# Two attention layers on one core: position products and q's transposes moved to the middle of score blocks, v's bias and two sums rearranged

## The chip, the cores and the metric

The kernel runs on one core of one Trainium2 chip. The metric is device time in microseconds, the median of several executions; lower is better. One execution was also profiled, and every duration below comes from that profile. The engines are named as the profile names them: PE is TensorE (PEld its weight loads), DVE is VectorE, ACT is ScalarE, POOL is GpSimd, SP issues most of the DMAs.

## The reference

Four images of 32x32 positions and 768 channels pass through two attention layers, each with 12 heads of 64 channels. Cut to what matters:

```python
def layer0(x):                       # x: (4, 1024, 768), after a group norm without weights
    q, k, v = heads(x@Wq + bq), heads(x@Wk + bk), heads(x@Wv + bv)
    attn = q @ k.T / 8 + rel_h(q)[..., None] + rel_w(q)[..., None, :]
    return softmax(attn) @ v  @ Wp + bp
def layer1(x):
    q, k, v = (layer_norm(dwconv3x3(s)) for s in split(x @ w_qkv.T + b_qkv))   # per head
    attn = q @ k.T / 8 + rel_h(q) + rel_w(q)
    return (softmax(attn) @ v + q) @ w_proj.T + b_proj
x = x + layer0(group_norm(x));  x = x + layer1(group_norm(x))
```

`rel_h` and `rel_w` are products of each query with a table of relative positions, 32 rows and 32 columns per query, added to every score.

## The kernel before, in words

**Stages and pairs.** The work is cut into eight stages (image, layer), in the order (0,0), (1,0), (0,1), (1,1), (2,0), (3,0), (2,1), (3,1), and each stage into six pairs of heads [...]. That makes 48 pairs, numbered 0 to 47: pairs 0 to 11 and 24 to 35 are of layer 0, the others of layer 1. All arithmetic is fp32.

**The run of a pair.** `attend` computes one pair's softmax attention for 1024 queries. It goes through four blocks: two halves of 512 queries (chunk c), and in each half two groups of four key tiles (g = 0 and 4). A block is: four score tiles (each four `s<-q,k` and two `s<-bias,ones` matmul records, the latter adding the relative positions), each followed by an `e` exponential on ACT over 128x1024 values; sums of the four exponentials into `acc` on DVE; then sixteen `av` matmul records that apply the exponentials to `vt`. Score tiles have two PSUM buffers, so the third tile of a block needs the first exponential done.

**A half's tail.** When a half's second block is over, ACT copies `av` to `weighed`, and the parts `sums` (a `z` matmul pair on PE, then `t`, Ln and Exp on ACT) and `result` (DVE: two Newton operations, then the product with `weighed`, put in place of q) are queued in `rest`. `more()` takes the next part of `rest`, once after the scores of each block and once after its `av`.

**Making the next pair meanwhile.** `attend` is a generator with four yields in a block, two after the scores and two after `av`; each yield is one step, so a run has 16. While pair i-1 runs, the pieces of pair i are emitted at the steps that `Pair.plan` gives, steps 4k and 4k+1 after the scores of block k, 4k+2 and 4k+3 after its `av`. All of PE, DVE, ACT and POOL work in exactly the order in which the program emits (a manual schedule). So the plan is the only scheduler: an instruction that waits holds up all behind it on its engine.

- Layer 0 (from pair 2 on): `sevens(Q)` makes the q and k products of a pair by a seven-product scheme from sums of quarters of the tokens (`mix_tokens`, DVE, in `quarters` and in place in `xn`), `sevens(V)` those of v for two pairs.
- Layer 1: `padded` (product of 24 matmul records `qkv`, then ACT writes a padded image), `taps` (nine DVE operations of 1.3 us), `centre` (32 `ln_c` records; ACT squares and copies), `squares` (a DVE reduction), `norm` (Ln and Exp on ACT, then DVE), `back` (four transposes `ln_t`, then ACT writes q and the reordered copy `q_t`, or k). The padded q of pair i+1 begins in the second half of run i-1, at its steps 8 and 10.
- Both: `positions(0)` and `positions(1)` (128 short `rel` records each, then two ACT copies into `whole`), and `split` (ACT casts `whole` to `high`, DVE subtracts, POOL issues 16 DMAs that spread both into the `bias` tiles).

**PSUM.** Two score tiles take four banks, `av` one, and the other three are one ring: every `bank(...)` call takes the next of the three, whatever it is for (`z`, `qkv`, `ln_c`, `ln_t`, `rel`, `proj` ...), and its first matmul waits until the tile three calls earlier has been read.

**Projection.** `project` handles a finished stage during the first run of the next: six output tiles, each with two halves of 24 `proj` records; DVE adds bias and residual. For image 0 each output tile first computes `pbias`, the projection of v's bias plus the projection's bias (12 records of one column), in both layers.

Of the kernel before, what the change touches and what calls it, by code (L numbers as in the profile page):

```python
# [45 lines left out]
def two_layers(ctx: ExitStack, tc: tile.TileContext, keep, x_in, wqkv, wproj, rels, windows, vrow, small, const, onehot, picks, out):  # L46
# [231 lines left out]
    sk = fixed.tile([P, NSMALL], F32, tag="sk", name="sk")  # L278
    nc.vector.tensor_scalar(sk, sm, SCALE, None, ALU.mult)

    pbias = fixed.tile([P, 2, NC], F32, tag="pbias", name="pbias")

    ones = fixed.tile([P, T], F32R, tag="ones", name="ones")
    plain = one.tile([P, T], F32, tag="whole", name="plain")
# [8 lines left out]
    class Pair:  # L293
# [253 lines left out]
        def plan(self):  # L547

            Q, K, V = 0, 1, 2
            if not self.layer and not in_sevens(self.i):  # L550
                return [
                    (0, lambda: self.plain(Q, 0)),
                    (2, lambda: self.plain(Q, 1)),
                    (4, lambda: self.plain(K, 0)),
                    (5, lambda: self.positions(0)),
                    (6, lambda: self.plain(K, 1)),
                    (7, lambda: self.positions(1)),
                    (8, lambda: self.plain_v(0)),
                    (10, lambda: self.split()),
                    (10, lambda: self.plain_v(1)),  # L560
                ]
            if not self.layer:
                pieces = [
                    (0, lambda: self.sevens(Q, False)),
                    (2, lambda: self.sevens(Q, True)),
                    (6, lambda: self.positions(0)),
                    (8, lambda: self.positions(1)),
                    (10, lambda: self.split()),
                ]
                if self.hp % 2 == 0:  # L570
                    pieces += [(8, lambda: self.sevens(V, False)), (10, lambda: self.sevens(V, True))]
                return [(r + shift(self.i), piece) for r, piece in pieces]

            pieces = [
                (-8, lambda: self.padded(Q, 0)),
                (-6, lambda: self.padded(Q, 1)),
                (-4, lambda: self.padded(K, 0)),
                (-2, lambda: self.padded(K, 1)),
                (2, lambda: self.padded(V, 0)),
                (4, lambda: self.padded(V, 1)),  # L580
                (3, lambda: self.centre(Q)),
                (5, lambda: self.squares(Q)),
                (7, lambda: self.norm(Q)),
                (8, lambda: self.centre(K)),
                (9, lambda: self.back(Q, 0)),
                (9, lambda: self.back(Q, 1)),
                (10, lambda: self.squares(K)),
                (10, lambda: self.positions(0)),
                (11, lambda: self.positions(1)),
                (12, lambda: self.norm(K)),  # L590
                (12, lambda: self.split()),
                (13, lambda: self.centre(V)),
                (14, lambda: self.back(K, 0)),
                (14, lambda: self.back(K, 1)),
                (14, lambda: self.squares(V)),
                (15, lambda: self.norm(V)),
            ]

            taps = (
                (Q, -4, (2, 2, 2, 2, 1)),  # L600
                (K, 2, (2, 2, 2, 2, 1)),
                (V, 8, (2, 2, 3, 2)),
            )
            for s, r, counts in taps:
                lo = 0
                for n in counts:
                    pieces.append((r, lambda s=s, lo=lo, n=n: self.taps(s, lo, lo + n)))
                    r, lo = r + 1, lo + n
            return pieces


# [2 lines left out]
    def attend(pair, os):  # L614
# [12 lines left out]
        for c in range(T // QC):  # L627
# [24 lines left out]
            def result(weighed, t, inv, cols=cols):  # L652

                nc.vector.scalar_tensor_tensor(t, t, -1.0, inv, ALU.mult, ALU.mult)
                nc.vector.scalar_tensor_tensor(inv, t, 2.0, inv, ALU.add, ALU.mult)

                if pair.layer:
                    nc.vector.tensor_tensor(inv, weighed, inv, ALU.mult)
                    nc.vector.scalar_tensor_tensor(q[:, cols], inv, col(LN + 4), q[:, cols], ALU.mult, ALU.add)
                else:  # L660
                    nc.vector.tensor_tensor(q[:, cols], weighed, inv, ALU.mult)

            for g in range(0, NKT, 4):
                es = []
                for kt in range(g, g + 4):
                    keys = slice(kt * P, (kt + 1) * P)
                    ps = ps_s.tile([P, 2, QC], F32, tag="s", name="s")
                    for j, rows in enumerate(heads):
                        nc.tensor.matmul(ps[:, j, :], k[rows, keys], q[rows, cols], start=True, stop=False)  # L669
                    for j, rows in enumerate(heads):  # L670
                        nc.tensor.matmul(  # L671
                            ps[:, j, :], ones[rows, keys], bias[c][rows, kt // 2, :],
                            start=False, stop=True,
                        )
                    e = work.tile([P, 2, QC], F32, tag="e", name="e", bufs=4)
                    nc.scalar.activation(e, ps, AF.Exp)  # L676
                    es.append(e)
                more()
                if g == 0:
                    av = ps_av.tile([P, QC], F32, tag="av", name="av")  # L680
                    acc = work.tile([P, 2, QC], F32, tag="acc", name="acc", bufs=1)
                    nc.vector.tensor_tensor(acc, es[0], es[1], ALU.add)  # L682
                for e in es[2 * (g == 0) :]:
                    nc.vector.tensor_tensor(acc, acc, e, ALU.add)  # L684
                yield
                yield
                for t, e in enumerate(es):
                    kt = g + t
                    for j in range(2):
                        nc.tensor.matmul(  # L690
                            av[j * D : (j + 1) * D, :], pair.vt[:, kt, j * D : (j + 1) * D], e[:, j, :],
                            start=(kt == 0), stop=(kt == NKT - 1),
                        )
                more()
                if g + 4 == NKT:
                    rest.extend((sums, result))
                    found = (copy(av), acc)
                yield
                yield

    def project(stage, os):

        b, layer = stage
        src, dst = rows(mid[b] if layer else x_in[b]), rows(out[b] if layer else mid[b])
        for m in range(NC):
            w = wp.tile([P, NC, P], F32, tag="wproj", name="wproj_t")
            nc.sync.dma_start(w, wproj[layer, :, :, m, :].rearrange("h p q -> p h q"))
            bias = col(BIAS[layer] + 18 + m)
            if b == 0:
                ps = bank("pbias")  # L710
                for n in range(NC):
                    v_bias = col(LN + 5) if layer else col(BIAS[0] + 12 + n)
                    nc.tensor.matmul(ps[:, 0:1], w[:, n, :], v_bias, start=(n == 0), stop=(n == NC - 1))
                nc.vector.tensor_tensor(pbias[:, layer, m : m + 1], ps[:, 0:1], bias, ALU.add)
            bias = pbias[:, layer, m : m + 1]
            for h in range(2):
                cols = slice(h * HALF, (h + 1) * HALF)
                x = wp.tile([P, HALF], F32, tag="x", name="x")
                nc.sync.dma_start(x, src[:, m, cols])
                ps = bank("proj")  # L720
                for n in range(NC):
                    halves(ps, w[:, n, :], os[n][:, cols], n == 0, n == NC - 1)
                nc.vector.scalar_tensor_tensor(x, ps, bias, x, ALU.add, ALU.add)  # L723
                nc.sync.dma_start(dst[:, m, cols], x)
                yield
# [2 lines left out]
    events = {}  # L728

    def at(step, piece):  # L730
        events.setdefault(step, []).append(piece)

    n_steps = NKT * (T // QC)
    oss = [[] for _ in stages]
    for k in range(1, len(stages)):
# [5 lines left out]
        if stages[k][1] == 0:  # L741
            mix = mix_tokens(stages[k])
            for r in range(5):
                at(first + 5 * n_steps + r - (0 if stages[k - 1][1] else 8), lambda mix=mix: next(mix, None))
        elif stages[k - 1][1] == 0:
            at(first + 4 * n_steps + 6, lambda: [nc.gpsimd.memset(pad, 0.0) for pad in pads])
    mix = mix_tokens(stages[0])
# [18 lines left out]
    for step in sorted(e for e in events if e < 0):  # L766
        for piece in events.pop(step):
            piece()
    step = 0
    for i, pair in enumerate(pairs):  # L770
        for _ in attend(pair, oss[i // NC]):
            for piece in events.pop(step, ()):
                piece()
            step += 1
    for part in rest:
        found = part(*found)
    def check():
# [306 lines left out]
```

## Time and profile before

| what | value |
|---|---|
| median of 3 runs | 4043.13 us (4043.02 to 4044.55) |
| the profiled execution's own time | 4040.44 us |
| its span in the profile | 4038.7 us, TensorE clock 0.996 of full |
| PE busy | 3945.2 us, 98% |
| DVE, ACT, POOL busy | 62%, 45%, 10% |
| scores | 3072 records `s<-q,k` and 1536 `s<-bias,ones`, 768 tiles |
| exponentials | 768 on ACT, 1023 ns each |
| `rel` | 12288 records of 195 ns in 96 groups |

How to read it: matmul records overlap, so a record's duration is not its price. The price of a group is the time from its first start to the next group's first start on PE; a score tile costs 1.19 us so measured, an `av` group 3.43, a `qkv` product 5.15 to 5.30, a `rel` group 1.22. What such a group takes beyond its usual price is lost time, even where the page shows no idle PE.

### The profile page before, as it was taken

What the parts mean: (1) busy time and instruction counts of PE and PEld (TensorE: products, weight loads), DVE (VectorE), ACT (ScalarE), POOL (GpSimd) and SP (SyncE); (2) the same over time, 40 slices, a digit from 0 to 9 for tenths busy, and PEclk for the clock granted to TensorE, in tenths of its full rate; (3) what the DMA queues carried; (4) which work ended last, traced back from release to release, by engine and by line L of the source; (5) the groups of instructions that cost most, each with busy time, mean ns of one, the idle gap of its engine ahead of it and who ended that gap; (6) DMA issues with size and microseconds to landing.
All of it is one profiled execution on the core that took longest, in us unless ns stands there. A gap on an engine that the chain in (4) does not pass through costs nothing.

```text
span 4038.7 us, 79929 instructions
## 1 busy us (share of the span) xinstructions
PE 3945.2 (98%) x35098; PEld 1720.3 (43%) x35098; DVE 2494.3 (62%) x2800; ACT 1812.1 (45%) x2669; POOL 409.8 (10%) x776
## 2 busy tenths in 40 slices
PE   7999999999999999999899999999999999999999
PEld 3534444434344444444444344354343444434443
DVE  2455423558489985799633454245575898848883
ACT  2444424545255553455423544244443555525552
POOL 0111100110000110010011110001100011000010
PEclk9999999999999999999999999999999999999999
DMA  5333242221411222212133222422114112131112
GB/s 160 85 112 113 71 128 73 57 65 38 132 48 38 76 52 75 63 49 69 41 103 88 58 70 63 144 58 70 47 53 127 37 43 53 40 104 43 38 47 75
DMA packets 179046, 293.34 MB, mean 73 GB/s; under 512 B 22528, under 2 KB 77952, under 8 KB 178688
## 3 DMA queue, kind: packets, MB, share of 16 engines
q1 hardware_dynamic: 117248, 187.41, 14.8%
q0 software_dynamic: 61440, 100.71, 10.9%
q8 instruction: 279, 4.57, 0.5%
q14 instruction: 79, 0.65, 0.1%
HBM read 153.36 MB, written 34.01 MB: 46 GB/s over the span
## 4 chain that ended last, share of the span: by engine, by line
PE 85%; DVE 8%; ACT 3%; issue 1%; DMA 1%; POOL 0%; DVEq 0%; SPq 0%; ACTq 0%
PE qkv L85 18%; PE av L690 14%; PE s L669 14%; PE proj L85 12%; PE m3m L85 4%; PE m4m L85 4%; PE m1m L85 4%; PE s L671 3%; PE ln_c L85 3%; PE rel L517 3%; PE z L639 2%; DVE shared L459 2%; DVE acc L684 2%; PE m L85 2%; ACT e L676 2%
## 5 line engine op out<-in xcount | busy, mean ns | idle before, releaser
L676 ACT ACTIVATE e<-s 128x1024 f32<-128x1024 f32 x768 | 781.3, 1023 | 529.8 <-PE s L671 503.7
L669 PE MATMUL s<-q,k 64*128 64x512 f32 x3072 | 831.8, 618 | 27.9 <-ACT e L676 22.2
L684 DVE TENSOR_TENSOR acc<-acc,e 128x1024 f32<-128x1024 f32 x576 | 705.4, 1225 | 184.4 <-ACT e L676 133.4
L85 PE MATMUL qkv<-xn,wqkv_t 128*64 128x512 f32 x3648 | 815.6, 596 | 2.8 <-DVE xn L268 2.6
L459 DVE SCALAR_TENSOR_TENSOR shared<-shared,sm 128x1056 f32<-128x1056 f32 x576 | 758.3, 1316 | 14.9
L671 PE MATMUL s<-bias,ones 64*128 64x512 f32 x1536 | 615.6, 794 | 13.9 <-DMA bias<-whole 9.5
L690 PE MATMUL av<-e,vt 128*64 128x512 f32 x2624 | 594.5, 595 | 0.0
L544 POOL DMA_DIRECT2D bias<-high x384 | 204.1, 552 | 3356.5 <-ACT high L533 3097.9
L85 PE MATMUL proj<-q,wproj_t 128*64 128x512 f32 x2304 | 504.9, 593 | 0.0
L85 PEld LDWEIGHTS qkv<-xn,wqkv_t 128*64 128x64 f32 x3648 | 252.9, 137 | 488.5 <-issue 482.6
L669 PEld LDWEIGHTS s<-q,k 64*128 64x128 f32 x3072 | 255.4, 186 | 362.0 <-ACT e L676 210.6
L442 ACT ACTIVATE shared<-qkv,sm 128x512 f32<-128x512 f32 (+1 forms) x288 | 129.2, 501 | 595.6 <-PE qkv L85 595.6
L723 DVE SCALAR_TENSOR_TENSOR x<-proj,pbias,x 128x512 f32<-128x512 f32 x96 | 72.1, 751 | 439.4 <-PE proj L85 435.0
L690 PEld LDWEIGHTS av<-e,vt 128*64 128x64 f32 x2624 | 184.7, 137 | 347.5 <-issue 328.9
L682 DVE TENSOR_TENSOR acc<-e 128x1024 f32<-128x1024 f32 x96 | 117.6, 1225 | 345.4 <-ACT e L676 344.6
L85 PEld LDWEIGHTS proj<-q,wproj_t 128*64 128x64 f32 x2304 | 163.7, 137 | 313.5 <-issue 311.7
L671 PEld LDWEIGHTS s<-bias,ones 64*128 64x128 f32 x1536 | 150.2, 188 | 199.6 <-issue 193.6
L544 POOL DMA_DIRECT2D bias<-whole x384 | 204.9, 562 | 119.5 <-DVE whole L534 109.0
L632 ACT COPY weighed<-av 128x512 f32<-128x512 f32 x96 | 56.3, 586 | 329.2 <-PE av L690 329.2
L85 PEld LDWEIGHTS ln_c<-cst,shared 128*64 128x64 f32 x2304 | 131.4, 138 | 44.4 <-issue 34.6
L517 PEld LDWEIGHTS rel<-q,rel 64*32 64x32 f32 x6144 | 111.6, 105 | 78.0 <-issue 61.0
L85 PE MATMUL ln_c<-cst,shared 128*64 128x128 f32 x2304 | 139.2, 274 | 3.1 <-DVE shared L459 3.1
(119 smaller groups left out, 3613.0 us busy)
## 6 DMA issues: line engine op xcount, KB each, us to landing
bias<-high POOLq DMA_DIRECT2D x384, 128.0 KB, 2.8
bias<-whole POOLq DMA_DIRECT2D x384, 128.0 KB, 3.0
wqkv_t<-in_wqkv SPq DMA_DIRECT2D x78, 384.0 KB, 3.1
wqkv_t<-mixed SPq DMA_DIRECT2D x66, 384.0 KB, 3.1
wproj_t<-in_wproj SPq DMA_DIRECT2D x48, 384.0 KB, 3.7
wqkv_t<-in_wqkv SPq DMA_DIRECT2D x66, 192.0 KB, 2.5
xn<-in_x SPq DMA_DIRECT2D x24, 512.0 KB, 7.8
x<-in_x SPq DMA_DIRECT2D x48, 256.0 KB, 2.8
```

The source lines that it names most:

```text
L85: nc.tensor.matmul(ps[lo : lo + D], a[:, lo : lo + D], b, start=start, stop=stop, **kw)
L442: nc.scalar.activation(self.pad[s][:, rows, there : there + src.shape[2]], src, AF.Identity, bias=col(self.column(s)))
L459: nc.vector.scalar_tensor_tensor(y, window, tap, y, ALU.mult, ALU.add)
L517: nc.tensor.matmul(ps[lo : lo + S, k * S : (k + 1) * S].rearrange("p (b c) -> p b c", b=2), rel[rows, 2 * self.layer + i, first : first + ...
L544: nc.gpsimd.dma_start(sets, some.unsqueeze(1).to_broadcast([D // 2, 2, QC]))
L639: nc.tensor.matmul(z[j * D : (j + 1) * D, :], cst[:, ONES : ONES + D], acc[:, j, :], start=True, stop=True,)
L669: nc.tensor.matmul(ps[:, j, :], k[rows, keys], q[rows, cols], start=True, stop=False)
L671: nc.tensor.matmul(ps[:, j, :], ones[rows, keys], bias[c][rows, kt // 2, :], start=False, stop=True,)
L676: nc.scalar.activation(e, ps, AF.Exp)
L682: nc.vector.tensor_tensor(acc, es[0], es[1], ALU.add)
L684: nc.vector.tensor_tensor(acc, acc, e, ALU.add)
L690: nc.tensor.matmul(av[j * D : (j + 1) * D, :], pair.vt[:, kt, j * D : (j + 1) * D], e[:, j, :], start=(kt == 0), stop=(kt == NKT - 1),)
```

## The change

It has six parts.

1. `attend` yields three times in a block: after the second score tile, after the scores, after `av`. The loop that empties the events runs the event "block - 0.5" at the first, steps 4k and 4k+1 at the second, 4k+2 and 4k+3 at the third. Whole-numbered steps thus stay where they were; a step 4k-0.5 falls in the middle of the scores of block k.
2. Layer 0: `positions(0)` goes from step 6 to 3.5 (middle of block 1), `positions(1)` from 8 to 7.5 (middle of block 2), `split` from 10 to 8.
3. Layer 1: both `back(Q)` go from step 9 to 7.5 (middle of block 2), both `positions` from 10 and 11 to 11.5 (middle of block 3). `squares(Q)` goes from 5 to 3, behind the taps of that step, `norm(Q)` from 7 to 5.
4. v's bias in layer 0: `result` leaves the quotient in `inv`, and a third part of the tail, `finish`, adds the bias on ACT while writing q. `pbias` is computed for layer 1 alone.
5. `mix_tokens` for stage (2,0), which follows a stage of layer 1, is emitted at steps 0, 0, 0, 1, 1 of the run before it instead of 0, 1, 2, 3, 4: with the new loop, all five sums after the scores of block 0.
6. `inv` thereby stays in use until the next block's scores.

```diff
@@ Pair.plan, layer 0
-                    (6, lambda: self.positions(0)),
-                    (8, lambda: self.positions(1)),
-                    (10, lambda: self.split()),
+                    (3.5, lambda: self.positions(0)),
+                    (7.5, lambda: self.positions(1)),
+                    (8, lambda: self.split()),
@@ Pair.plan, layer 1
-                (5, lambda: self.squares(Q)),
-                (7, lambda: self.norm(Q)),
+                (5, lambda: self.norm(Q)),
                 (8, lambda: self.centre(K)),
-                (9, lambda: self.back(Q, 0)),
-                (9, lambda: self.back(Q, 1)),
+                (7.5, lambda: self.back(Q, 0)),
+                (7.5, lambda: self.back(Q, 1)),
                 (10, lambda: self.squares(K)),
-                (10, lambda: self.positions(0)),
-                (11, lambda: self.positions(1)),
+                (11.5, lambda: self.positions(0)),
+                (11.5, lambda: self.positions(1)),
...
+            pieces.append((3, lambda: self.squares(Q)))
             return pieces
@@ attend
                 else:
-                    nc.vector.tensor_tensor(q[:, cols], weighed, inv, ALU.mult)
+                    nc.vector.tensor_tensor(inv, weighed, inv, ALU.mult)
+                return (inv,)
+
+            def finish(inv, cols=cols):
+
+                if not pair.layer:
+                    nc.scalar.activation(q[:, cols], inv, AF.Identity, bias=col(pair.column(2)))
...
                     nc.scalar.activation(e, ps, AF.Exp)
                     es.append(e)
+                    if kt == g + 1:
+                        yield
                 more()
...
                 yield
-                yield
                 for t, e in enumerate(es):
...
-                    rest.extend((sums, result))
+                    rest.extend((sums, result, finish))
                     found = (copy(av), acc)
                 yield
-                yield
@@ project
-            if b == 0:
-                ps = bank("pbias")
-                for n in range(NC):
-                    v_bias = col(LN + 5) if layer else col(BIAS[0] + 12 + n)
-                    nc.tensor.matmul(ps[:, 0:1], w[:, n, :], v_bias, start=(n == 0), stop=(n == NC - 1))
-                nc.vector.tensor_tensor(pbias[:, layer, m : m + 1], ps[:, 0:1], bias, ALU.add)
-            bias = pbias[:, layer, m : m + 1]
+            if layer:
+                if b == 0:
+                    ps = bank("pbias")
+                    for n in range(NC):
+                        nc.tensor.matmul(ps[:, 0:1], w[:, n, :], col(LN + 5), start=(n == 0), stop=(n == NC - 1))
+                    nc.vector.tensor_tensor(pbias[:, m : m + 1], ps[:, 0:1], bias, ALU.add)
+                bias = pbias[:, m : m + 1]
@@ events
-                at(first + 5 * n_steps + r - (0 if stages[k - 1][1] else 8), lambda mix=mix: next(mix, None))
+                at(first + 5 * n_steps + (r // 3 if stages[k - 1][1] else r - 8), lambda mix=mix: next(mix, None))
...
-    step = 0
+    block = 0
     for i, pair in enumerate(pairs):
-        for _ in attend(pair, oss[i // NC]):
-            for piece in events.pop(step, ()):
-                piece()
-            step += 1
+        for n, _ in enumerate(attend(pair, oss[i // NC])):
+
+            for step in ((block - 0.5,), (block, block + 1), (block + 2, block + 3))[n % 3]:
+                for piece in events.pop(step, ()):
+                    piece()
+            block += 4 * (n % 3 == 2)
```

More of the change, by code (lines that the diff above doesn't have):

```diff
@@ L279, in two_layers @@
     nc.vector.tensor_scalar(sk, sm, SCALE, None, ALU.mult)
-    pbias = fixed.tile([P, 2, NC], F32, tag="pbias", name="pbias")
+    pbias = fixed.tile([P, NC], F32, tag="pbias", name="pbias")
     ones = fixed.tile([P, T], F32R, tag="ones", name="ones")
```

## The prediction

> **What bounds the kernel now.** I read the page first: its engine shares and the 40 slices.
>
> ```profile
> PE 3945.2 (98%) x35098; PEld 1720.3 (43%) x35098; DVE 2494.3 (62%) x2800; ACT 1812.1 (45%) x2669; POOL 409.8 (10%) x776
> PE   7999999999999999999899999999999999999999
> ```
>
> PE is busy in all slices but the first, so only three things can pay: less PE work, cheaper transitions between kinds of PE work, and the waits of PE that are left. Next, the waits of PE alone (columns: waiting group, releaser, us in total, times, longest).
>
> ```profile
> PE s L669 <- ACT e L676: 22.2, 43, 1.8
> ...
> PE s L671 <- DMA bias<-whole: 9.5, 4, 2.9
> ...
> PE m4m L85 <- DVE xn L234: 5.9, 2, 5.5
> ...
> PE ln_t L495 <- ACT shared L473: 1.8, 2, 0.9
> ```
>
> The first line understates: matmul ends are modelled, so a short wait hides under the record before. I therefore took start-to-start times from the timeline, for all 768 score tiles. Free, a tile costs 1.19 us. The second tile of a block costs more, because the third needs the first exponential: 1.28 where ACT is free, 1.63 where ACT was still copying `rel` when the block began. Here is the start of block 3 in the run of pair 41 (timeline; start, duration, engine, line), PE and then ACT:
>
> ```profile
> 3474.48 1.03 PE L669 MATMUL s<-q,k 64*128 64x512 f32 x4
> ...
> 3476.11 1.13 PE L669 MATMUL s<-q,k 64*128 64x512 f32 x4 [0.36 <-ACT e L676]
> ```
>
> ```profile
> 3461.81 0.78 ACT L410 ACTIVATE q<-ln_t,sm 128x512 f32<-128x512 f32 x1
> 3462.47 1.27 ACT L411 ACTIVATE q_t<-ln_t,sm 128x512 f32<-128x512 f32 x1
> 3463.52 0.76 ACT L410 ACTIVATE q<-ln_t,sm 128x512 f32<-128x512 f32 x1
> 3464.15 1.27 ACT L411 ACTIVATE q_t<-ln_t,sm 128x512 f32<-128x512 f32 x1
> ...
> 3473.40 0.58 ACT L522 COPY whole<-rel 64x512 f32<-64x512 f32 x1 [0.32 <-PE rel L517]
> 3473.99 1.01 ACT L523 COPY whole<-rel 64x512 f32<-64x512 f32 x1
> 3475.03 1.94 ACT L676 ACTIVATE e<-s 128x1024 f32<-128x1024 f32 x2
> ```
>
> The two copies (1.6 us) push the exponential to 3475.03, and the third tile starts at 3476.11 instead of 3475.67: 0.44 us lost. The first four ACT lines matter below: the two `back(Q)` occupy ACT for 3.6 us (3461.81 to 3465.42).
>
> [...] `av` (128 rows) costs 3.43 us before another 128x64 group and 3.53 to 3.58 before scores or `rel`; `qkv` 5.15 against 5.25 to 5.30; `rel` 1.10 before `rel`, 1.22 before anything else. [...] ACT's order is that of the program, and exponentials stand behind copies as above. [...] The timeline shows a ring wait in the run of pair 22:
>
> ```profile
> 1917.47 0.66 PE L495 MATMUL ln_t<-cst,shared 128*128 128x128 f32 x4
> 1919.05 0.66 PE L495 MATMUL ln_t<-cst,shared 128*128 128x128 f32 x4 [0.92 <-ACT shared L473]
> ```
>
> The second transpose group needs the bank of the first `ln_c`, which ACT left at 1918.99.
>
> **The change, part by part.** Gains are negative.
>
> *Layer 0's v bias.* Removed: six `pbias` groups of 1.43 us on PE (1611.61 to 1613.04 for one of the same shape), each with one mode switch of 0.1: 6 x 1.5 = **-9.0**. The six DVE additions (0.16 us) are hidden. Added: 48 ACT operations 128x512 with a bias column. Nearest row: L410 from `shared`, 721 ns[...]. 48 x 0.72 = 35 us of ACT, emitted behind the fourth exponential of blocks 1 and 3, where ACT next has only `weighed`, after 3.4 us of `av`. Its wait on DVE's `result`, half a block old, is over. So 0; if DVE were late by over 2 us, the 0.72 would delay the next first exponential, up to 35 us in all. I take 0.
>
> *Layer 0's positions.* In the middle, the 1.22 us of `rel` cover the first exponential. q and `q_t` precede the block's exponentials on ACT, so `rel` does not wait. The excess of the second tile in these blocks, added over the runs: block 1 2.9 (21 x 0.14), block 2 10.2 (mostly 0.44, up to 0.90), one block 3 0.5: **-13.6**. Switches: `av` before scores instead of `rel` 0.05, `z` before `sevens` instead of `rel` 0.91 for 1.01: 22 x 0.15 = **-3.3**. The third and fourth exponential come up to 0.4 us later (copies 1.6 us); `av` needs them 1.7 and 2.6 us after it starts, about 1.2 us to spare.
>
> *`split` at 8.* ACT's cast and DVE's subtraction go before `sevens(V)`. On ACT the chain from the block's start is copies to 5.4, exponentials to 7.6, `t`, Ln, Exp to 9.7, cast to 10.8, `sevens`' copy to 11.4; PE wants that bank at 12.2: 0. In the run of pair 3, DVE is held by `mix_weights` (its V group takes 15.0 instead of 10.5): +1.2. POOL's 16 DMAs keep their order; those for the second half still wait for block 3's scores, and the `memset` of the pads still precedes them. Pairs 5 and 29 now wait 2.1 us each for `bias<-whole`, because three or four sums of quarters precede DVE's subtraction; only one will: **-4.2**.
>
> *Quarters' sums.* `m4m` waits 5.5 us for the fourth sum, which ran at 1965.12 to 1966.88 behind four `result` operations (2.9 us). Now it precedes them: **-2.8**. The fifth is also ahead of `result`: block 1's `acc` is 1.8 us later, which the seven-product group covers.
>
> *Layer 1, an ordinary run* (pair 41 as the model; block 2 begins at 3448.18, called T; blocks 2 and 3 take 25.11 + 22.00 = 47.11). New order on PE: two tiles 2.38, both `back` 1.02 + 0.1 for the switch, two tiles 2.38, `z` 0.91, `ln_c` 1.75, `qkv` 5.20, `av` 3.43, `qkv` 5.28: 22.45. Block 3: 2.38, both `rel` 2.32, 2.38, `qkv` 5.15, `ln_c` 1.75, `av` 3.53, `ln_t` 1.02, `qkv` 5.30: 23.83. Sum 46.28, -0.83 before new waits.
>
> Is DVE's `norm(Q)` there? Its `squares` end at 3446.18; moved up behind step 3's taps, where ACT's squares are ready, they leave `norm` (2.1 us) next behind the taps that precede them: T + 0.1. PE wants it at T + 2.4. 2.3 us to spare.
>
> The new wait is the ring. Banks are now drawn as back, back, `z`, `ln_c`, `ln_c`, `qkv`: `qkv` needs `z`'s bank, as before, but ACT reads `z` only after its queue: exponentials to T + 3.5, the q copies 3.6 us to 7.15, two exponentials to 9.1, `t` 0.60 to 9.7. (Before: `t` at 3454.16 to 3454.76, T + 6.6.) PE is ready at 2.38 + 1.12 + 2.38 + 0.91 + 1.75 = T + 8.54. It waits **1.2 us**, and `av` and all else behind it. Bounds: 0 if ACT's copies overlapped better than measured, 2 if the accumulator read (0.19) and a later start of the copies count. Net +0.37 a run. It needs a q product of a next layer-1 pair behind `z`: 22 runs. In 19, 19 x 0.37 = **+7.0**. In three (pairs 14, 20, 38) DVE also has 2.7 us of `bn_stats` before `norm`: 2.5 us of waiting replaces the old 1.8, the ring wait shrinks to 0.6, net 3 x 0.15 = **+0.5**. The runs of pairs 22 and 46 have little PE work and DVE decides; ACT's later exponentials put it back 0.9 us, and the `bias` of the next pair with it: 2 x 1 = **+2.0**.
>
> In block 3 the copies (3.2 us) delay two exponentials to 9 us after its start; `av` comes at 14. Covered. DVE's `acc` ends 1 to 2 us later in both blocks; it idles 8.2 us a run.
>
> **Sum:** -9.0 - 13.6 - 3.3 + 1.2 - 4.2 - 2.8 + 7.0 + 0.5 + 2.0 = **-22.2**. From the profiled execution's 4040.44 us this gives 4018; the median of the runs stands 2.7 higher, so 4043.1 - 22 = **4021**. About 0.2% (8 us) is what a measurement can tell from no change.
>
> **Rivals.**
> A. *No ring wait*: ACT keeps pace. Against it: the 3.6 us are measured [...]. The 1.2 us go in 19 runs and 0.6 in three: another -25, **3996**.
> B. *DVE late at the middle of block 2 (slower)*: PE stands at `ln_t` for `norm(Q)` with both remaining score tiles behind it. For it: pairs 14, 20, 38, and pairs 16, 22 and 40, where `squares` end 1.45 us later. Against: 8.2 us idle a run. Lateness beyond the spare 2.3 us counts in 22 runs, less 0.55 that the ring wait gives back. It decides at 2.3 + 0.55 + 22.2/22 = 3.9 us; with 4.5 us, 22 x 1.65 = 36, **4057**.
> C. *The middle covers nothing*: the third tile's wait moves to the fourth tile or to `av` behind later exponentials. Then layer 0's 16.9 are not gained: **4038**. Against: 1.2 us to spare at `av`.
>
> **How the numbers follow.** My forecast 0.56, A 0.14, B 0.18, C 0.12. My forecast's own range is 4008 to 4034, from the ring wait's 0 to 2 us and 3 us either way in layer 0. The range, 4000 to 4053, leaves out half of A and a part of B. Faster by over 0.2% takes my forecast (nearly all) and A, 0.68; the same C and a rest, 0.14; slower B, 0.18.
>
> **What would show it.** Right: second tiles of 1.19 us before `rel` and `ln_t`; no layer-0 `pbias`; a new PE wait `qkv` <- ACT `t`, some 20 times, near 1.2 us; blocks 2 and 3 at 47.5 in ordinary layer-1 runs and about 0.8 us less per layer-0 run. Wrong: `ln_t` waiting for DVE in most layer-1 runs, waits of `av` on `e` in layer 0, or no wait behind `z`.

## The result, and the profile after

The changed kernel takes **4074.01 us** (median of 4 runs, 4072.05 to 4076.71); the kernel before takes 4043.84 (median of 4, 4043.02 to 4045.61). The ratio is 1.0074, 95% interval 1.0057 to 1.0092: slower by 0.7%, where 0.6% faster was forecast. The profiled execution of after took 4076.71 us, with a span of 4074.9, against 4040.44 and 4038.7 before.

From the page of after come its engine shares, PE's slices and the queue that brings instructions (packets, MB, share of 16 DMA engines):

```profile
PE 3941.4 (97%) x35026; PEld 1727.5 (42%) x35026; DVE 2493.4 (61%) x2794; ACT 1828.3 (45%) x2717; POOL 406.8 (10%) x776
...
PE   7999999999999999999899999999999999999999
...
q8 instruction: 279, 4.57, 0.5%
```

The row of slices is that of before, digit for digit. PE is busy 3.8 us less, and the span is 36.2 us longer. (The medians lie 30.2 us apart: the profiled execution of after is the slowest of its four, that of before lies under its median.) So PE stands still more. The waits of PE in after say where (waiting group, releaser, us in total, times, longest):

```profile
PE rel L517 <- issue: 37.0, 19, 2.7
...
PE qkv L85 <- ACT t L646: 15.4, 20, 0.8
PE ln_c L85 <- DVE shared L459: 11.8, 2, 7.1
...
PE ln_t L495 <- DVE shared L488: 7.0, 3, 2.3
PE s L675 <- ACT e L682: 4.7, 4, 2.0
...
PE s L677 <- DMA bias<-whole: 3.9, 2, 2.4
...
PE m4m L85 <- DVE xn L234: 3.0, 2, 2.7
PE s L675 <- issue: 2.8, 3, 2.1
```

Nearly every line but the two with "issue" is one that the prediction named: the 43 waits for the first exponential are 4, the ring wait `qkv` <- `t` is there 20 times, `ln_t` waits for DVE only in three runs, `m4m` waits half as long, and the two waits of `ln_c` lie in the runs of pairs 22 and 46, where DVE was to decide. The lines with "issue" are those that it didn't name. "issue" means that PE waited for nothing that the profile shows.

Here is one such wait, in block 3 of the run of pair 41, where the prediction had shown the start of before (timeline, PE):

```profile
3490.68 1.13 PE L675 MATMUL s<-q,k 64*128 64x512 f32 x4
...
3491.88 1.02 PE L675 MATMUL s<-q,k 64*128 64x512 f32 x4
...
3493.05 0.21 PE L517 MATMUL rel<-q,rel 64*32 64x32 f32 x1
...
3497.67 0.21 PE L517 MATMUL rel<-q_t,rel 64*32 64x32 f32 x1 [2.20 <-issue]
...
3498.02 2.08 PE L675 MATMUL s<-q,k 64*128 64x512 f32 x4
3499.11 1.42 PE L677 MATMUL s<-bias,ones 64*128 64x512 f32 x2
3500.32 1.40 PE L675 MATMUL s<-q,k 64*128 64x512 f32 x4
...
3501.88 5.37 PE L85 MATMUL qkv<-xn,wqkv_t 128*64 128x512 f32 x24
```

The first two tiles have their 1.19 us. The two `rel` groups begin at 3493.05 and give way to the third tile at 3498.02: 4.97 us for 2.32 of work, with a hole of 2.20 near the end of the second group. After the hole the third tile takes 2.30 us instead of 1.19. ACT shows that no exponential was late and that it, too, had nothing to do (timeline, ACT):

```profile
3492.08 2.12 ACT L682 ACTIVATE e<-s 128x1024 f32<-128x1024 f32 x2 [0.38 <-PE s L677]
3494.39 0.58 ACT L522 COPY whole<-rel 64x512 f32<-64x512 f32 x1 [0.19 <-PE rel L517]
...
3498.14 0.58 ACT L522 COPY whole<-rel 64x512 f32<-64x512 f32 x1 [2.10 <-PE rel L517]
```

Both exponentials were done at 3494.2, so the score buffers were free; the second copy waits 2.10 us for PE. And the slow tile? The same stretch cut into windows (PE and PEld busy with records, then the other engines, the granted clock, the DMA share, GB/s):

```profile
3494.00:3495.40 1.40, 1.40 (x155) 1.33 (x142) 1.30 (x2) 1.20 (x3) 0.00 (x0) 1.00 0.06 12
3495.40:3497.60 2.20, 0.07 (x9) 0.00 (x0) 0.89 (x1) 0.64 (x1) 0.00 (x0) 1.00 0.00 0
...
3498.00:3499.00 1.00, 1.00 (x7) 0.50 (x4) 0.00 (x0) 0.85 (x2) 0.00 (x0) 0.50 0.08 16
...
3502.00:3503.00 1.00, 1.00 (x6) 0.36 (x8) 0.85 (x1) 1.00 (x2) 0.00 (x0) 1.00 0.00 0
```

In 1.4 us PE worked on 297 records, matmuls and weight loads together; then none began for 2.2 us; after that the clock stood at 0.50 until about 3501.1. The DMA view of 3493 to 3499 has, for the instruction queue:

```profile
q8 instruction: 2, 0.03, 2.7%
```

Two packets of 16 KB. In the trace's DMA records one starts at 3494.99 and takes 1.27 us, and PE goes on at 3497.67, 2.7 us after its start; the next starts at 3498.81.

**The sum over the runs of pairs** (from a run's first score to the next one's, in the two profiled executions, 36.2 us apart). In the 24 runs that make a layer-1 pair (runs of pairs 11 to 22 and 35 to 46), 2083.1 us became 2147.9: +64.8, predicted +9.5. In the other 23, 1789.2 became 1760.2: -29.0, predicted -31.7. The mistake is 55 us and lies in layer 1, and there in block 3. The means over the twelve ordinary runs (those without group-norm work or a stage's change; blocks 0 and 1 keep their 16.20 and 13.59 us):

| kernel | block 2, us | block 3, us |
|---|---|---|
| before | 25.11 | 22.00 |
| predicted for after | 23.65 | 23.83 |
| after | 23.28 | 26.79 |

### The profile page after: what moved, and what is told of

It reads as the page before. It is cut to its first block, busy times and chain, and to the rows that moved or that the text cites. A ratio compares the mean times of both kernels' runs of the same rounds, so it can differ in the third digit from the quotient of the medians.

```text
span 4074.9 us, 79979 instructions
## 1 busy us (share of the span) xinstructions
PE 3941.4 (97%) x35026; PEld 1727.5 (42%) x35026; DVE 2493.4 (61%) x2794; ACT 1828.3 (45%) x2717; POOL 406.8 (10%) x776
## 4 chain that ended last, share of the span: by engine, by line
PE 86%; DVE 7%; ACT 3%; issue 2%; DMA 1%; POOL 0%; DVEq 0%; SPq 0%; ACTq 0%
PE qkv L85 19%; PE s L675 16%; PE av L697 14%; PE proj L85 12%; PE m3m L85 4%; PE m1m L85 4%; PE m4m L85 4%; PE s L677 4%; PE rel L517 3%; DVE acc L692 2%; PE m L85 2%; PE ln_c L85 2%; PE z L639 2%; DVE shared L459 2%; ACT e L682 1%
## 5 line engine op out<-in xcount | busy, mean ns | idle before, releaser
L675 PE MATMUL s<-q,k 64*128 64x512 f32 x3072 | 842.7, 624 | 11.1 <-ACT e L682 4.7
L85 PE MATMUL qkv<-xn,wqkv_t 128*64 128x512 f32 x3648 | 816.3, 597 | 18.7 <-ACT t L646 15.4
L729 DVE SCALAR_TENSOR_TENSOR x<-proj,pbias,x 128x512 f32<-128x512 f32 x48 | 36.0, 751 | 209.0 <-PE proj L85 209.0
L729 DVE SCALAR_TENSOR_TENSOR x<-proj,sm,x 128x512 f32<-128x512 f32 x48 | 36.0, 751 | 207.9 <-PE proj L85 203.3
```

Source lines behind the costliest of these rows:

```text
L85: nc.tensor.matmul(ps[lo : lo + D], a[:, lo : lo + D], b, start=start, stop=stop, **kw)
```

## The experiments

**Theory F**: PE runs out of instructions. 35,026 matmuls and as many weight loads in 279 packets, each of 16,384 bytes, are 251 records a packet. A `rel` group is 128 of each, 256 instructions in 1.2 us; two back to back are 512 in 2.4 us, and the next packet would come later than that. **Rival M**: the loss belongs to the middle of a block, not to the neighbourhood of the two groups.

The trace of before holds a hint for F. Its waits have a line of the same kind, and its timeline shows both places:

```profile
PE rel L517 <- issue: 4.0, 2, 2.1
```

```profile
1927.34 0.19 PE L517 MATMUL rel<-q_t,rel 64*32 64x32 f32 x1 [2.09 <-issue]
...
3910.94 0.19 PE L517 MATMUL rel<-q,rel 64*32 64x32 f32 x1 [1.90 <-issue]
```

They lie in the runs of pairs 22 and 46, the only two of before in which no other PE work stands between the `rel` groups.

| kernel | median, us (range) | ratio to before (95%) |
|---|---|---|
| b_adjacent | 4105.77 (4100.39 to 4108.73) | 1.0155 (1.0139 to 1.0172) |
| apart | 4028.08 (4023.38 to 4031.35) | 0.9960 (0.9946 to 0.9974) |
| near | 4024.06 (4023.19 to 4030.25) | 0.9956 (0.9939 to 0.9972) |
| l0_only | 4014.96 (4014.35 to 4019.45) | 0.9932 (0.9916 to 0.9949) |
| half | 4017.09 (4015.42 to 4019.41) | 0.9934 (0.9918 to 0.9951) |
| near_ring | 4006.93 (4004.60 to 4012.02) | 0.9915 (0.9898 to 0.9931) |
| bias_only | 4031.70 (4029.09 to 4038.87) | 0.9976 (0.9965 to 0.9986) |

The kernel before took 4043.92 beside the first four and 4043.01 beside the last three.

**b_adjacent: the kernel before, with only the neighbourhood added.** Both groups stand outside the scores.

```diff
@@ before, layer 1
                 (10, lambda: self.positions(0)),
-                (11, lambda: self.positions(1)),
+                (10, lambda: self.positions(1)),
```

> The kernel before, with one step changed: in layer 1 positions(1) goes from step 11 to 10, so that both rel groups (512 PE instructions with their weight loads) stand back to back behind av, not in the middle of scores. Theory F (PE runs out of instructions: a packet of the instruction queue is 16 KB, 256 PE instructions, and two rel groups use two of them in 2.4 us): the second group waits 2 to 2.7 us for issue in most of the 24 layer-1 runs; 4043.8 + 24 x 2.3 - 3 = 4096, between 4080 and 4105. Rival M (the loss comes of crowding ACT in the middle of a block: 3.2 us of copies ahead of two exponentials): nothing is in the middle here, a little is saved on mode switches, 4037 to 4044, no issue wait.

Measured: 4105.77, 61.9 us slower. Its waits of PE begin with

```profile
PE rel L517 <- issue: 47.2, 22, 2.7
```

The wait needs no middle. One line of the plan, with not one instruction more, costs 1.5%. Block 2, in which the groups now stand, takes 27.72 us instead of 25.11. M falls. F's number was 10 us short, and the measured time lies 0.8 us above its range.

**apart: after, with the first group taken away from the second.** It goes behind the `av` of block 2.

```diff
@@ after, layer 1
-                (11.5, lambda: self.positions(0)),
+                (10, lambda: self.positions(0)),
                 (11.5, lambda: self.positions(1)),
```

> The changed kernel, with layer 1's positions(0) at step 10 (behind av of block 2) instead of 11.5; positions(1) stays in the middle of block 3. Theory F: a qkv product of 5 us stands between the two rel groups, the issue wait is gone, blocks 2 and 3 of an ordinary layer-1 run take 24.6 + 22.7 us instead of 23.3 + 26 to 28; 4025, between 4016 and 4034. Rival M: ACT still has one pair of copies ahead of the two exponentials, about half of the loss stays; 4045 to 4060.

Measured: 4028.08. One group stays in the middle of block 3, and no wait on "issue" is left. Block 3 is at 22.78. The time lies in F's range and 17 us below M's.

**near: after, with just the last two score tiles between the groups.**

```diff
@@ after, layer 1
                 (11.5, lambda: self.positions(0)),
-                (11.5, lambda: self.positions(1)),
+                (12, lambda: self.positions(1)),
```

> The changed kernel, with layer 1's positions(1) at step 12 (after the scores of block 3) and positions(0) still in the middle: two score tiles, 2.4 us of PE, stand between the rel groups. Theory F: the fetch that took about 2.7 us from its start to the next instruction is now mostly covered; the wait falls from 2.2 to between 0 and 1 us a run; 4020 to 4042. Rival M: as in the run with the groups further apart, half of the loss stays; 4045 to 4060.

Measured: 4024.06. Of the waits on "issue" this is left:

```profile
PE rel L517 <- issue: 0.4, 2, 0.3
```

Two tiles, 2.4 us with 24 instructions, are distance enough here, though not by much: by an estimate from 1.10 us of `rel` and 2.38 of tiles, a packet's 256 instructions now last about 3.5 us. Block 3 is at 24.07 on average. M, with 4045 or more, falls here too.

**half: the two groups stay neighbours, with half the instructions in each.** In layer 1 one record does two rows of the image, and the second of them uses the window of the first: the kernel leaves out every second window of relative positions.

```diff
@@ after, positions
-            for k in range(S // 2):
+            n = 2 if self.layer else 1
+            for k in range(0, S // 2, n):
...
-                    by_row = image(self.q[rows])[:, :, at, :]
+                    by_row = image(self.q[rows])[:, :, at : at + n, :].rearrange("p b a c -> p a b c")
...
```

> The changed kernel with layer 1's rel products made for two rows of the image at a time: half as many rel instructions (64 matmul records and 64 weight loads a group) of twice the length, in the same two back-to-back groups in the middle of block 3, with the same ACT copies. It leaves out every second window of relative positions in layer 1 (the second row of each two uses the first one's). Theory F (instructions): both groups together are one packet of 256 instructions instead of two, the issue wait is gone, block 3 takes about 24 us; 4018, between 4008 and 4032. A rival that blames the place, the adjacency or the copies, and not the number of instructions, keeps 4065 to 4078.

Measured: 4017.09. The instructions that write or read `rel` show that layer 1's records are of 64 columns and half as many:

```profile
L518 PE MATMUL rel<-q,rel x4608: 192/196/240, 37.7 to 3888.2; 64*32 64x32 f32 x128, 64*32 64x64 f32 x64
```

Place, order, neighbourhood and bytes written are those of after, and its waits have no "issue" line at all. By these counts each of the 24 layer-1 pairs has 128 matmuls and as many weight loads fewer, 256 instructions. The two groups together take 1.92 us, where after's take 4.19 on average (2.32 + 44.9/24). So the records of double width are also 0.4 us cheaper than 2.32; the other 1.9 us are the hole. Block 3 falls from 26.79 to 23.48. So the number of instructions in the stretch decides: place, order and PSUM banks are the same in both kernels, and a theory built on one of these would keep the loss.

**l0_only: the layer-0 parts, the bias and the quarters, with layer 1's plan as it was.**

```diff
@@ after, layer 1 (as in before)
-                (5, lambda: self.norm(Q)),
+                (5, lambda: self.squares(Q)),
+                (7, lambda: self.norm(Q)),
...
-                (7.5, lambda: self.back(Q, 0)),
-                (7.5, lambda: self.back(Q, 1)),
+                (9, lambda: self.back(Q, 0)),
+                (9, lambda: self.back(Q, 1)),
...
-                (11.5, lambda: self.positions(0)),
-                (11.5, lambda: self.positions(1)),
+                (10, lambda: self.positions(0)),
+                (11, lambda: self.positions(1)),
...
-            pieces.append((3, lambda: self.squares(Q)))
```

> The changed kernel with layer 1's plan as it was before (back at 9, positions at 10 and 11, squares at 5, norm at 7); layer 0's positions, its v bias on ACT and the quarters' sums stay changed. Both theories put the whole loss in layer 1's plan: by the sums of block times layer 0's part is worth 29 us, so 4015, between 4010 and 4021. If ACT's added bias or the new loop itself cost time, it stays above 4035.

Measured: 4014.96, 29.0 less than before. The waits for the first exponential that layer 1 keeps are

```profile
PE s L675 <- ACT e L682: 16.8, 25, 2.0
```

So the change's layer-0 side is worth 29.0 of the 31.7 us that the prediction gave it, and its layer-1 side, as written, costs 59.

**near_ring: near, and `centre(K)` behind `qkv`.** In near, the two `ln_c` groups take the two banks after `z`, so `qkv` must have `z`'s own. With `qkv` first it takes the bank that the first `back(Q)` left, and a whole product lies between `z` and the group that needs its bank.

```diff
@@ after, layer 1
-                (8, lambda: self.centre(K)),
+                (9, lambda: self.centre(K)),
...
-                (11.5, lambda: self.positions(1)),
+                (12, lambda: self.positions(1)),
```

> The changed kernel with positions(1) of layer 1 at step 12 (as in the run where only that was changed, 4024.1) and with centre(K) at step 9, that is behind padded(Q) of the next pair: the product then takes the bank that the first back(Q) left, and the two ln_c groups come 5 us later. Ring theory: the wait of qkv for t, 0.95 us in 22 runs, goes and no other takes its place; 4024.1 - 21 = 4003, between 3998 and 4010. If something else held that product (ACT's or DVE's lateness rather than the ring of three banks), it waits as before: 4020 to 4028.

Measured: 4006.93, 17.1 below near: the fastest of all, 0.85% faster than before and 1.6% than after. Block 2 of after in the run of pair 41, and then the same place in near_ring (timelines, PE):

```profile
3473.18 1.08 PE L639 MATMUL z<-acc,cst 128*64 128x512 f32 x4
3474.09 1.92 PE L85 MATMUL ln_c<-cst,shared 128*64 128x128 f32 x32
3476.80 5.37 PE L85 MATMUL qkv<-xn,wqkv_t 128*64 128x512 f32 x24 [0.79 <-ACT t L646]
```

```profile
3420.58 1.08 PE L639 MATMUL z<-acc,cst 128*64 128x512 f32 x4
3421.49 5.32 PE L85 MATMUL qkv<-xn,wqkv_t 128*64 128x512 f32 x24
3426.64 1.92 PE L85 MATMUL ln_c<-cst,shared 128*64 128x128 f32 x32
3428.38 3.60 PE L697 MATMUL av<-e,vt 128*64 128x512 f32 x16
```

In the first, 2.71 us pass between `ln_c` and `qkv` where `ln_c` is worth 1.75; in the second, nothing waits. Block 2 goes from 23.27 (near) to 22.27, against 22.45 in the sum without the ring wait.

**bias_only: before, with v's bias by ACT alone** (and so `pbias` for layer 1 only, as in the change).

```diff
@@ before
-                    nc.vector.tensor_tensor(q[:, cols], weighed, inv, ALU.mult)
+                    nc.vector.tensor_tensor(inv, weighed, inv, ALU.mult)
+                return (inv,)
...
+            def finish(inv, cols=cols):
...
-                    rest.extend((sums, result))
+                    rest.extend((sums, result, finish))
...
```

> The kernel before with the v bias of layer 0 alone changed: 48 ACT operations of 0.72 us added behind the scores, 72 pbias matmul records removed. My step said -9.0 us on PE and nothing on ACT: 4035, between 4032 and 4038. If ACT's 35 us counted, 4044 or more.

Measured: 4031.70, 11.3 less than before (by the interval, 6 to 14). In its profile the 23 runs that make no layer-1 pair are 8.0 us shorter, the others the same to 0.1. The 48 operations on ACT cost nothing that can be seen.

## Why the prediction was wrong

**The step that failed** is the sum for layer 1's block 3: "Block 3: 2.38, both `rel` 2.32". It priced two neighbouring groups, 1.10 and 1.22 us, as if PE had its instructions at hand. What stands in its place:

- *The hole.* Added over the 24 places, two neighbouring groups take 44.9 us more than 2.32 each; the two places of before take 4.4 more. That is +40.5.
- *The clock.* In the 22 runs other than those of pairs 22 and 46, the trace of before has no stretch of half clock, after has ten, each 3.41 us. Eight of them begin in block 3, in the `rel` groups or within 1.5 us behind them; the mean granted clock is 0.992 in after and in b_adjacent, 0.996 in before. Less the 2.1 us that fall into the groups themselves, the eight make 25 us. If PE does half its work in them, as the tile of 2.30 us for 1.19 suggests, that is up to +13. This is an estimate from the records of one execution; no run separates it from the hole, and the mean of half, which has no wait for "issue", is 0.992 too (apart 0.994, near 0.995, near_ring 0.996). The other two, in the runs of pairs 14 and 38, begin in block 2, where `ln_t` had stood 2.32 us for DVE. They are up to +3, and belong to DVE's lateness.

Together about 56, against 55 us that the prediction missed.

**Is it the packets?** The traces settle it further. Number PE's instructions in the order of their starts, weight loads and the few others included. At all 17 stops of over 1 us in after's `rel` groups and at the two of before, the first instruction behind the stop leaves the same remainder, 193, when its number (from 0) is divided by 256. Take these places as the borders of packets. At the 17, a border falls 75 to 246 instructions into the 512. The next packet starts 0.7 to 1.6 us after that border, and PE stops at the following border until 2.2 to 2.8 us after the packet's start. From border to border that makes 3.0 to 4.1 us, where 256 instructions of `rel` last 1.1. At the other seven places the first border falls within the first 30 instructions, and the last packet had started 1.1 to 4.7 us before the groups began. There PE stops for 0.6 us at most in the groups, though in the run of pair 42 it stops 2.1 us right behind them, in a wait of `s` for "issue".

The sizes agree: all 279 packets of after have 16,384 bytes, and at 251 records a packet they come close to the 256 of the remainders. Where 256 instructions of `rel` come at a time, PE hardly waits for "issue" there: 0.4 us in near, and not at all in apart and half. Where 512 are used up in 2.4 us, it stops for up to 2.7. As for the clock, at 3497.7 it fell to 0.50 at the end of 2.2 us without work.

**Step by step**, by the prediction's own terms:

- *Layer 0's v bias*, -9.0: measured -8.0 in the profile of bias_only, where the run of pair 6, which held these `pbias`, is 9.0 shorter. ACT had the room. Right.
- *Layer 0's positions and switches*, -13.6 and -3.3: in the run of pair 8, as an example, blocks 1 and 2 lose 0.15 and 0.60 us, and over the 23 runs that make no layer-1 pair, without those of pairs 3, 6 and 23, the two blocks lose 17.5. Right: no `av` waits for an exponential, and rival C (nothing gained) is out.
- *`split` at 8 in the run of pair 3*, +1.2: measured +2.5. Too small; `m3m`'s longest wait for DVE went from 2.9 to 5.7.
- *Bias waits of pairs 5 and 29*, -4.2: did not come. The waits for `bias<-whole` went from four to two (3.9 us above), but the exponential then waits for the `acc` sums to free its buffer, and a score tile for that: two of the four `s` <- `e` waits, up to 2.0 us. In the run of pair 29 the place takes 29.81 instead of 29.65.
- *Quarters' sums*, -2.8: `m4m`'s longest wait went from 5.5 to 2.7, the run of pair 23 lost 3.2. Right.
- *Layer 1's block 2*, 22.45 and a ring wait of 1.2: measured 23.28. The mechanism is the one named, 20 times. It measures 0.95 by start-to-start and 0.77 by the waits (15.4/20). The term was a quarter too large.
- *Three runs with group-norm work*, `ln_t` late by 2.5 us in each: it waits 7.0 us in the three, 2.3 each. But the net of 3 x 0.15 was too small: in near, where the hole is gone, they are 0.8, 0.8 and 2.4 us longer than before.
- *Runs of pairs 22 and 46*, +1 each: +1.4 and +1.9.

With the `rel` groups apart and nothing else altered (near), layer 1's plan costs 4024.06 - 4014.96 = 9.1 us over l0_only; the prediction's terms 7.0 + 0.5 + 2.0 are 9.5, and near's 4024 lies 3 us from the 4021 that was forecast for after. That is in part luck: in near's profile the 24 runs are 12.0 us longer than before, 5.5, 4.1 and 2.4 by these terms, and the other runs and the two ends make up for it.

**The rivals.** A, no ring wait, is the right mechanism for another kernel: taking it away in near_ring brought 17.1 us where A had 25. B, DVE late at `ln_t`, gave the right sign for a reason that is not there: DVE is late in three runs, not in 22. The chance of slower stood on B alone. The actual cause was in none of the cases, so the range could not reach it.

**What could have been read ahead.** The page of before has the two numbers of F, 279 packets and twice 35,098 instructions. And PE's waits of before have "issue: 4.0, 2, 2.1" for `rel`: two stops of 2 us each, at the two places where the groups were neighbours already. The prediction took its 1.10 for a `rel` group before another from these same two places, the only ones of the kind, and said nothing of the stop in the second group, while the change made 22 more such places.

## What to carry to other kernels

Count instructions as well as microseconds: when many short matmuls are moved together, see how long a packet's 256 instructions last. In this kernel 1.1 us stopped PE for up to 2.7, and about 3.5 us (the estimate for near) hardly did, for 0.4 in all. Keep longer matmuls between such groups, or make fewer and longer ones. A wait on "issue" in the profile before is a price tag: find where it occurs, and ask whether the change makes more such places. When a plan is moved to hide one engine's latency, also look whose bank or buffer the next piece in the ring draws.

## What the runs showed of the hardware

- From the start of an instruction packet to PE's next instruction, 2.7 us pass in the run of pair 41, of which the DMA takes 1.27; at the 17 long stops of after it is 2.2 to 2.8 us. 256 short instructions of `rel` last 1.2 us; one group at a time was covered (no wait for "issue" in apart), of two neighbours the second was not (37.0 us in 19 waits in after). The longest stop was 2.7 us by the waits.
- The stop can cost again: eight times in after, TensorE's clock stood at 0.50 for 3.41 us from within the two groups or up to 1.5 us behind them. At 3497.7 that began at the end of 2.2 us without work.
- The order alone of the same instructions is worth 62 us in b_adjacent. The page of after, 30 us slower than before, shows the same slices of PE as that of before, with a 9 in nearly every place.
